# A ConvNeXt block whose convolution output is turned by VectorE out of PSUM, with the norm's mean and weights folded into the first matrix

## The chip, the cores and the metric

The kernel runs on one core of a Trainium2 chip. A core has five engines that run side by side, each through its own queue, in order: TensorE (PE, matrix products into PSUM, with a separate weight load, PEld), VectorE (DVE), ScalarE (ACT), GpSimd (POOL) and SyncE (SP, which here only issues DMAs). The metric is the device time of one launch in microseconds, the median of several runs. All data are 32-bit floats.

## The reference

The input is 32 images of 384 channels and 28 by 28 pixels. Cut to what matters:

```
y  = depthwise_conv_7x7(x, dw_w, padding 3) + dw_b        # each channel on its own
mu, var = mean and variance of y over the 384 channels, per pixel
y  = (y - mu) * rsqrt(var + 1e-6) * ln_g + ln_b
y  = gelu(y @ w1 + b1)                                    # 384 -> 1536
gx = sqrt(sum over pixels of y*y);  nx = gx / (mean over features of gx + 1e-6)
y  = grn_g * (y * nx) + grn_b + y
x1 = x + y @ w2 + b2                                      # 1536 -> 384
avg, mx, mn = mean, max, min of x1 over the pixels, per channel
out = sigmoid(small_gate(avg, mx, mn) + x1)
```

## The kernel before

**Convolution stage.** The 384 channels are walked in 48 steps (`s`) of 8 channels. An image is cut into 7 strips (`j`) of 4 rows, padded to 32 columns, so that a strip is 128 values; `turn_x` (L452) brings the strips onto the 128 partitions by 128x128 transposes on TensorE, and DVE or ACT copies them from PSUM into `xt`. For each channel `conv` (L580) multiplies all 7 x 32 = 224 strips by three blocks of a banded matrix `tmat` that holds the 49 weights (L599, L601, L603). The result of two channels lies in one PSUM bank, `pc` (4 banks rotate), with (row, column) of the strip on the partitions and (strip, image) along the free axis. One pair is read out by ACT (L615), the next by DVE (L607), each time adding the bias `dwb`, into `yc`, an SBUF tile of 16 channels (two buffers), which `store` (L623) writes to `yd` in DRAM every second step. SP issues, in order, the load of `tmat` three steps ahead (L406), the loads of x (L433), the stores of `yc` and the stores of `u` (L753).

In the same stage POOL forms two matrices in `form_w` (L518, lines L524 and L526): the two matrix products are carried out by schemes with fewer products, which multiply sums of weight blocks (`UPSTEPS`, `STEPS`) with sums of input blocks (`FORMS`, `SUMS`). `form_w` writes each sum of weight blocks into one of three `u` buffers and stores it to DRAM; u1 (from w1) is formed from step U1 = 4 on, u2 (from w2) from step U2 = 22 on. w1 and then w2 lie in the same tile, `ws`, into which `later` (L699, L700) loads them at steps 2 and 19.

**From conv to blocks.** The last two steps are done twice: first for images 0 to 15, then for images 16 to 31. Beside the second half, `first_image` (L653) normalises and transposes image 0.

**Per image.** `load_y` (L271) fetches one image, pixels of a strip on the partitions, strips and channels along the free axis. `block_stats`, `stats` and `std` (L289, L279, L294) take mean and variance on DVE; `norm` (L793) applies them on ACT, strip by strip; `turn` (L802) transposes each 128x128 piece on TensorE (L816, 7 strips x 3 blocks = 21); `evac` (L818) copies from PSUM on ACT, multiplies by `ln_g` and adds `ln_b`, into `room_acc`, channels on the partitions. `forms_up` (L320) makes the sums of input blocks on POOL. `up` (L836) multiplies by w1 in 15 steps for each of 4 groups (L858); ACT and DVE gather the products from PSUM (L865 to L875); ACT applies Gelu (L828), squares and sums (L834) and scales (L308 through `affine`). `down` (L962) multiplies by w2 in 38 steps of 6 products (L986), with the operands' sums on POOL (L947); DVE adds the products to the image's x (L1001, L1003) and takes max and min of each quarter of a channel (L1008). `gate_store` (L1021) ends an image.

**Order.** The main loop calls `up(b + 1)` and then `down(b)`. What runs beside them hangs on their steps by two tables: `within` (L1070) for `up`, `beside` (L1124) for `down`. A planner puts each engine's instructions in an order from its own time estimates; `keep_in_program_order` pins an instruction behind what was written before it on its engine, `issue_after` pins a load behind an earlier one. Each engine then works through its queue in that order.

## Time and profile before

| | |
|---|---|
| median of 3 runs | 3089.75 us (3089.39 to 3091.18) |
| profiled execution: its span, first to last instruction | 3087.8 us; the page gives no other time for this execution, so its own time stands here as its span, 1.95 us under the median |
| mean granted TensorE clock | 0.997 |
| convolution stage | to about 493 us |
| one image in the middle of the main loop | 80.33 us |
| DMA in the convolution stage (24 to 480 us) | 355 GB/s, share 0.94 |
| DMA in the main loop | 189 GB/s, share 0.59 |

The profile gives each engine's busy time, the groups of equal instructions with their mean duration, the waits (which instruction waited for which), and the chain that ended last: from the last instruction back, at each step, to what released it. Matrix products are pipelined: the durations of two in a row overlap, so the cost of one on the path is read from the distance of two starts. A 32-bit product is recorded as two instructions.

### The profile page before, as it was taken

To read this page: it belongs to the slowest core of one execution; us is meant where nothing else is said; L and a number is where in the kernel's file an instruction comes from. 1 tells how busy PE (TensorE), PEld (TensorE's weight loads), DVE (VectorE), ACT (ScalarE), POOL (GpSimd) and SP (SyncE) were. 2 spreads that over 40 slices of the span, in tenths; PEclk is the share of its full clock that TensorE was granted. 3 is DMA by queue.
4 is the path that set the end of the run, shared out by engine and by line. 5 is a ranking of instruction groups with operands and counts; after the bars stand their busy time and mean duration, and the time that the engine had idled before them with its cause. 6 is when DMAs were issued, how large, how long until landed. Compare 5 with 4: busy or idle time off the path is not lost.

```text
span 3087.8 us, 45729 instructions
## 1 busy us (share of the span) xinstructions
PE 3055.8 (99%) x15011; PEld 2484.8 (80%) x15011; DVE 1992.4 (65%) x5382; ACT 1982.9 (64%) x3147; POOL 2265.9 (73%) x1767
## 2 busy tenths in 40 slices
PE   8999999999999999999999999999999999999998
PEld 8999997777777777777777777777777777777777
DVE  3444446666667777776666676666666666666766
ACT  3333335757777777777777777777777777777761
POOL 1233442798888888888888888888888888888897
PEclk9999999999999999999999999999999999999999
DMA  9999986455555555556565666655565555555546
GB/s 370 368 373 349 356 325 230 137 157 190 189 191 189 191 191 191 190 189 198 190 197 190 197 191 196 194 186 182 188 195 180 184 185 189 190 189 191 187 153 201
DMA packets 316132, 658.31 MB, mean 213 GB/s; under 512 B 127583, under 2 KB 142202, under 8 KB 306938
## 3 DMA queue, kind: packets, MB, share of 16 engines
q1 hardware_dynamic: 302916, 616.59, 60.7%
q10 hardware_dynamic: 12982, 38.80, 3.2%
q8 instruction: 122, 2.00, 0.3%
q14 instruction: 112, 0.92, 0.1%
HBM read 560.78 MB, written 94.53 MB: 212 GB/s over the span
## 4 chain that ended last, share of the span: by engine, by line
PE 94%; POOL 3%; DVE 1%; ACT 1%; DMA 1%; issue 0%; ACTq 0%; SPq 0%; POOLq 0%; DVEq 0%
PE ph_A L858 13%; PE ph_C L858 13%; PE ph_B L858 13%; PE pz_A L986 8%; PE pz_C L986 8%; PE pz_D L986 7%; PE pz_F L986 7%; PE pc L599 5%; PE pc L603 4%; PE pc L601 4%; PE py L816 2%; PE pt L460 2%; PE pz_H L986 2%; PE pz_I L986 2%; PE pz_E L986 2%; POOL d_room L947 1%
## 5 line engine op out<-in xcount | busy, mean ns | idle before, releaser
L947 POOL TENSOR_TENSOR d_room<-y 128x588 f32<-128x588 f32 x253 | 363.5, 1443 | 335.3 <-PE pz_B L986 187.6
L308 ACT ACTIVATE y<-y,fv,gsc 128x784 f32<-128x784 f32 x372 | 359.0, 1030 | 380.1 <-DVE gsc L894 380.1
L828 ACT ACTIVATE y<-y,fv 128x784 f32<-128x784 f32 x384 | 350.2, 945 | 186.4 <-DVE y L873 164.4
L858 PE MATMUL ph_A<-room,ws 128*128 128x392 f32 x1240 | 461.2, 494 | 0.8 <-ACT te L865 0.4
L858 PE MATMUL ph_C<-room,ws 128*128 128x392 f32 x1240 | 462.0, 495 | 0.0
L858 PE MATMUL ph_B<-room,ws 128*128 128x392 f32 x1240 | 458.8, 492 | 1.3 <-DVE yc L607 1.3
L947 POOL TENSOR_TENSOR d_room<-d_room,y 128x588 f32<-128x588 f32 x308 | 441.2, 1437 | 16.7
L858 PEld LDWEIGHTS ph_C<-room,ws 128*128 128x128 f32 x1240 | 232.9, 190 | 179.8 <-DVE y L871 20.6
L858 PEld LDWEIGHTS ph_A<-room,ws 128*128 128x128 f32 x1240 | 233.0, 190 | 178.8 <-ACT te L865 13.2
L858 PEld LDWEIGHTS ph_B<-room,ws 128*128 128x128 f32 x1240 | 234.6, 190 | 164.8 <-issue 1.5
L947 POOL TENSOR_TENSOR d_room<-y,d_room 128x588 f32<-128x588 f32 x214 | 307.6, 1437 | 44.9 <-PE pz_A L986 18.0
L834 ACT ACTIVATE junk<-y 128x784 f32<-128x784 f32 x384 | 329.0, 857 | 7.9
L343 POOL TENSOR_TENSOR room<-room 128x392 f32<-128x392 f32 x300 | 300.8, 1020 | 11.8
L947 POOL TENSOR_TENSOR y<-y 128x588 f32<-128x588 f32 x180 | 258.6, 1437 | 7.1
L867 DVE TENSOR_TENSOR y<-y,ph_C 128x392 f32<-128x392 f32 x384 | 214.4, 559 | 27.3
L1008 DVE TENSOR_REDUCE stq<-x 128x1 f32<-128x196 f32 x768 | 228.2, 349 | 5.5
L869 DVE TENSOR_TENSOR y<-y,ph_B 128x392 f32<-128x392 f32 x256 | 137.5, 557 | 143.5 <-ACT y L828 119.4
L615 ACT ACTIVATE yc<-pc,dwb 128x224 f32<-128x224 f32 (+1 forms) x200 | 103.5, 619 | 192.4 <-PE pc L603 183.9
L599 PE MATMUL pc<-xt,tmat 128*128 128x224 f32 (+1 forms) x800 | 213.6, 349 | 5.1 <-ACT xt L471 3.6
L986 PE MATMUL pz_A<-d_room,u 128*128 128x196 f32 x1050 | 203.5, 330 | 0.0
L524 POOL TENSOR_SCALAR u<-ws 128x384 f32<-128x384 f32 (+1 forms) x53 | 66.6, 1261 | 186.0 <-DMA u2d<-u 133.3
L469 DVE COPY xt<-pt 128x512 f32<-128x512 f32 (+1 forms) x184 | 112.0, 618 | 134.5 <-PE pt L460 134.4
(241 smaller groups left out, 6650.6 us busy)
## 6 DMA issues: line engine op xcount, KB each, us to landing
u<-u2d SPq DMA_DIRECT2D x487, 384.0 KB, 3.4
ws<-u1d SPq DMA_DIRECT2D x384, 320.0 KB, 3.0
tmat<-fs SPq DMA_DIRECT2D x47, 1420.0 KB, 11.6
ws<-u2d SPq DMA_DIRECT2D x121, 384.0 KB, 3.4
yd<-yc SPq DMA_DIRECT2D x22, 1792.0 KB, 6.7
yi<-yd SPq DMA_DIRECT2D x31, 1232.0 KB, 8.0
x<-in_x SPq DMA_DIRECT2D x32, 1176.0 KB, 5.6
out<-x ACTq DMA_DIRECT2D x31, 1176.0 KB, 7.1
```

The costliest lines, as they stand in the source:

```text
L308: eng.activation(out, in_, AF.Identity, bias=add, scale=mul)
L343: tc.keep_in_program_order(eng.tensor_tensor(d, o[in0], o[in1], op))
L599: keep(nc.tensor.matmul(po, t[:, c, P : 2 * P], xc, start=True, stop=False))
L601: nc.tensor.matmul(lo, t[:, c, 2 * P : T0 + MW], after, start=False, stop=False)
L828: nc.scalar.activation(y, y, AF.Gelu, bias=b1_t[:, f : f + 1], scale=1.0)
L834: nc.scalar.activation(junk, ys[b][:, f, :], AF.Square, accum_out=ssqs[b][:, f : f + 1])
L858: nc.tensor.matmul(banks[t, bk][:, :NH], wts[t][:, i % UG, :], o[opnd], start=(first == 1), stop=True, skip_group_check=True,)
L867: nc.vector.tensor_tensor(d, d, p, ALU.add)
L869: nc.vector.tensor_tensor(d, d, p, ALU.subtract)
L947: nc.gpsimd.tensor_tensor(d[0], o[a][0], o[c][0], ALU.add if sign == "+" else ALU.subtract)
L986: nc.tensor.matmul(pz[:, :NQ4], wt[:, i % UD, t, :], o[opnd][0][:, t, :], start=(first and t == 0), stop=(t == KD - 1), skip_group_check=True,
L1008: nc.vector.tensor_reduce(stq[:, v, m, h : h + 1], xh, AX.X, op2)
```

## The change

The convolution result stays unbiased in PSUM, and DVE turns it there in blocks of 32x32 (`nc.vector.transpose`): a block (32 columns of a row x 32 images) becomes (32 images x 32 columns), so `yt` holds (row in the strip, image) on the partitions and (channel, strip, column) along the free axis. `yt` has 8 channels and one more plane, the running sum over channels, which DVE's `sums_y` writes once a step; `yt` has two buffers and is stored every step. ACT squares `yt` with the bias added; POOL adds four squared channels at a time to `ssum`. At the end of the stage `finish` makes the reciprocal standard deviation of every pixel from the two sums, once for each half of the images, and stores it in `rsd`. `load_y` then fetches an image with the channels already on the partitions (three DMAs), and one row of reciprocal deviations spread over all partitions (a fourth, `rb`). `normed` adds the bias and multiplies by `rb` on DVE, three instructions an image, in place of the statistics, `norm`, `turn` and `evac`. The mean is not subtracted: `center_w` multiplies w1 by `ln_g` and takes its column means away, which removes the mean from the product, and adds `ln_b @ w1` to `b1`. It runs at the ends of steps 4 and 5; w1 is loaded at step 3 instead of 2, `fv` and `cv` (bias and norm vectors) at steps 1 and 2 instead of 4 and 5, w2 at 21 instead of 19; U1 and U2 move from 4 and 22 to 6 and 24. `form_w` starts with an addition where it can. Pixels of an image are now ordered by row in the strip, so `down` reads x with a stride of 112; max and min are taken once per channel (the last image excepted). The new pool `rbp` has one buffer.

```diff
+    yd = dram.tile([P, C, YR], F32, name="yd")
+    rsd = [dram.tile([P, YR], F32, name=f"rsd_{i}") for i in range(2)]
...
         with tc.issue_after(last_u2[-1]) if last_u2 else ExitStack():
-            nc.sync.dma_start(yk[:, : NY - NLAST], yd[:, :, b, :])
-        nc.sync.dma_start(yk[:, NY - NLAST :], yl[:, :, b, :])
...
+            for cb in range(CB):
+                load_y_part(b, yi, cb, 0, P)
+        base = rsd[0 if b < B0 else 1]
...
+                offset=base.offset + b * YR,
+                ap=[[0, P], [B * YR, NQD], [1, YR]],
...
+    def load_y_part(b, yi, cb, p0, p1):
+        nc.sync.dma_start(
+            yi[p0:p1, cb],
+            yd.rearrange("(q b) c n -> b c q n", b=B)[b, cb * P + p0 : cb * P + p1],
+        )
...
+    def normed(b, cbs=range(CB)):
...
+        for cb in cbs:
+            nc.vector.scalar_tensor_tensor(
+                accs[b][:, cb].rearrange("p (r w) -> p r w", w=HW), rows(yis[b][:, cb]),
+                dwb_t[:, cb : cb + 1], rows(rbs[b]), ALU.add, ALU.mult,
+            )
...
-        U1, U2 = 4, 22
+        U1, U2 = 6, 24
...
+            todo = sorted(terms(text), key=lambda x: -x[0])
+            blks = [(sg, wv[:, :, int(k), m, :]) for sg, m, k in todo]
+            if len(blks) > 1 and blks[0][0] > 0:
+                (_, a), (sg, c) = blks[:2]
+                nc.gpsimd.tensor_tensor(t, a, c, ALU.add if sg > 0 else ALU.subtract)
+                del blks[:2]
+            else:
+                nc.gpsimd.tensor_scalar(t, blks[0][1], float(blks[0][0]), None, ALU.mult)
+                del blks[:1]
+            for sg, blk in blks:
+                nc.gpsimd.tensor_tensor(t, t, blk, ALU.add if sg > 0 else ALU.subtract)
             stores.append((dst, t))
...
+        def center_w(part):
...
+                        nc.tensor.matmul(
+                            pb[:, f : f + 1], w1r[:, cb, f * P : (f + 1) * P],
+                            lnb_t[:, cb : cb + 1], start=(cb == 0), stop=(cb == CB - 1),
+                        )
+                nc.vector.tensor_tensor(b1f, pb[:, :FB], b1_t, ALU.add)
+                for cb in range(CB):
+                    nc.vector.tensor_scalar(
+                        w1r[:, cb], w1r[:, cb], lng_t[:, cb : cb + 1], None, ALU.mult
+                    )
+                return
+            f0 = (part - 1) * 4 * P
+            pm = psx.tile([P, 4, P], F32, tag="pt", name=f"pm_{part}")
+            pm = pm.rearrange("p a b -> p (a b)")
+            for cb in range(CB):
+                nc.tensor.matmul(
+                    pm, less, w1r[:, cb, f0 : f0 + 4 * P], start=(cb == 0), stop=(cb == CB - 1)
+                )
+            for cb in range(CB):
+                w = w1r[:, cb, f0 : f0 + 4 * P]
+                nc.vector.tensor_tensor(w, w, pm, ALU.add)
...
-            cy = cc % YC
-            if c2 % 2:
-                nc.vector.tensor_tensor(
-                    yc[:, b0:b1, :, cy : cy + 2].rearrange("p b j c -> p c j b"),
-                    pc[:, :, : NJ * nb].rearrange("p c (j b) -> p c j b", j=NJ),
-                    dwb[:, cc : cc + 2].unsqueeze(2).unsqueeze(3).to_broadcast([P, 2, NJ, nb]),
...
+            cy = 2 * c2
+            nc.vector.transpose(yt[:, cy : cy + 2, :], pc[:, :, :N])
...
+            for ci in range(2):
+                nc.scalar.activation(
+                    sq[:, cy % SQ + ci, :], yt[:, cy + ci, :], AF.Square,
+                    bias=dwb[:, cc + ci : cc + ci + 1], scale=1.0,
...
-            else:
-                for ci in range(2):
-                    nc.scalar.activation(
-                        yc[:, b0:b1, :, cy + ci].rearrange("p b j -> p j b"),
-                        pc[:, ci, : NJ * nb].rearrange("p (j b) -> p j b", j=NJ),
...
+            if cy % SQ == SQ - 2:
...
+                    nc.gpsimd.tensor_tensor(ssum, ssum, sq, ALU.add)
...
+            nc.vector.tensor_reduce(
+                dst, yt[:, n0:n1, :].rearrange("p c n -> p n c"), AX.X, ALU.add
...
+        def finish(yt, part, s2, half):
...
+            sums_y(s1, yt, TC - SQ, TC + 1)
+            nc.vector.tensor_reduce(s2r, s2.rearrange("p c n -> p n c"), AX.X, ALU.add)
+            nc.vector.scalar_tensor_tensor(mu, s1, dws, part, ALU.add, ALU.add)
+            nc.vector.scalar_tensor_tensor(s1, mu, 1.0 / C**2, mu, ALU.mult, ALU.mult)
+            nc.vector.scalar_tensor_tensor(va, s2r, 1.0 / C, s1, ALU.mult, ALU.subtract)
+            nc.vector.tensor_scalar(va, va, 0.0, EPS, ALU.max, ALU.add)
+            nc.scalar.activation(s2r, va, AF.Sqrt)
+            rs = s1
+            nc.vector.reciprocal(rs, s2r)
+            nc.scalar.dma_start(rsd[half], rs)
+            return rs
...
+                for q in range(NQD):
+                    nc.tensor.matmul(
+                        pr[q // 2][:, q % 2], ident[:, q * B : q * B + 1].to_broadcast([P, P]),
+                        rs, start=True, stop=True,
                     )
...
+                        nc.vector.scalar_tensor_tensor(
...
+                            rows(yis[0][:, cb, 2 * i : 2 * i + 2]),
+                            dwb_t[:, cb : cb + 1], rows(pr[i]), ALU.add, ALU.mult,
...
+                forms_up(0, nc.vector)
...
+                        nc.vector.memset(
+                            pcs[i][:, ci, :N].rearrange("p (j b) -> p j b", b=B)[:, :, B0:], 0.0
+                        )
...
+                                (nc.sync, nc.scalar)[q % 2].dma_start(
+                                    yd[
+                                        q * B + b0 : q * B + b1,
+                                        (NK - 2 + i) * TC : (NK - 1 + i) * TC, :,
+                                    ],
+                                    y2[i][q * B + b0 : q * B + b1, :TC, :],
+                                )
...
+                                sums_y(y2[1][:, TC, :], y2[0], 0, TC + 1)
...
+                            sums_y(part, y2[1], 0, TC - SQ)
...
+                first_image(2 * PAIRS, firsts["y"])
+                if B0 < B:
+                    finish(y2[1], part, ssum, 1)
...
+                nc.sync.dma_start(yd[:, s * TC : (s + 1) * TC, :], yt[:, :TC, :])
+                yn = new_yt(f"yt_{s + 1}")
+                sums_y(yn[:, TC, :], yt, 0, TC + 1)
...
+                nc.vector.tensor_reduce(dws, dwb, AX.X, ALU.add)
+            if U1 - 2 <= s < U1:
+                for part in ((0, 1), (2, 3))[s - U1 + 2]:
+                    center_w(part)
...
-                xh = xt[:, m, h * NQ4 : (h + 1) * NQ4]
+                xh = xt[:, m, :].rearrange("p (j q w) -> p q j w", q=NQD, w=HW)[:, NQD - 1 - h]
...
-                for v, op2 in ((1, ALU.max), (2, ALU.min)):
-                    nc.vector.tensor_reduce(stq[:, v, m, h : h + 1], xh, AX.X, op2)
...
+                elif not any(left[m, x] for x in "abcd"):
+                    for v, op2 in ((1, ALU.max), (2, ALU.min)):
+                        nc.vector.tensor_reduce(
+                            st[:, v * CB + m : v * CB + m + 1], xt[:, m, :], AX.X, op2
+                        )
...
+                at((0, 18), normed, 1)
...
-            for j in range(NJ):
-                at((0, 20 + j), block_stats, b + 1, j)
-            at((0, 28), stats, b + 1)
-            at((0, 28), std, b + 1)
-        if 1 <= b and b + 1 < B:
-            for j in range(3):
-                at((2, 24 + 2 * j), norm, b + 1, j)
...
-            for i, jj in ((0, (0, 1)), (3, (2, 3)), (7, (4, 5)), (TURNED, (6,))):
-                for j in jj:
-                    at(i, turn, b + 2, j)
-                for j in {0: (3, 4), 3: (5, 6)}.get(i, ()):
-                    at(i, norm, b + 2, j)
-                if i in (3, TURNED):
-                    at(i, evac, b + 2, i // TURNED)
+            for cb in range(CB):
+                at(2 + 3 * cb, normed, b + 2, (cb,))
```

## The prediction

> **What bounds the kernel now.** I read the page's span and chain first, to see which engine ends last; then busy time by stretches, one in the convolution stage and one whole image of the main loop; then the groups and waits that the change touches.
>
> ```profile
> span 3087.8 us, 45729 instructions
> ...
> PE 94%; POOL 3%; DVE 1%; ACT 1%; DMA 1%; issue 0%; ACTq 0%; SPq 0%; POOLq 0%; DVEq 0%
> ```
>
> ```profile
> 24.00:480.00 456.00, 454.48 (x2905) 441.24 (x2904) 187.92 (x301) 165.13 (x277) 164.41 (x155) 1.00 0.94 355
> 1120.39:1200.72 80.33, 80.33 (x374) 63.08 (x374) 55.65 (x158) 57.30 (x92) 65.67 (x51) 1.00 0.59 189
> ```
>
> The columns are length, then PE, PEld, DVE, ACT, POOL busy, granted clock, DMA share, GB/s. TensorE is the path in both stages; the others have slack (POOL 14.7 us of an image, DVE 24.7). In the convolution stage DMA is nearly full too. Next, what one transpose and one narrow product cost on PE, read from start to start:
>
> ```profile
> 1160.07 1.16 PE L986 MATMUL pz_A<-d_room,u 128*128 128x196 f32 x6
> 1161.07 0.49 PE L816 MATMUL py<-ident,yn 128*128 128x128 f32 x3
> 1161.39 1.16 PE L986 MATMUL pz_C<-d_room,u 128*128 128x196 f32 x6
> ...
> 1173.34 0.28 PE L886 MATMUL pg<-gs,ones_f 128*128 128x1 f32 x2
> 1173.48 1.24 PE L986 MATMUL pz_H<-d_room,ws 128*128 128x196 f32 x6
> ```
>
> Three transposes take 0.32 us of the path, 0.107 each; a product one column wide takes 0.14. Last, the groups of the convolution stage, the shared work of DVE and POOL, and POOL's wait:
>
> ```profile
> L816 PE MATMUL py<-ident,yn 128*128 128x128 f32 x651 | 92.1, 273 | 0.2
> L607 DVE TENSOR_TENSOR yc<-pc,dwb 128x448 f32<-128x448 f32 x92 | 85.6, 932 | 143.4 <-PE pc L603 134.7 <-ACT yc L615 4.0 <-PE pt L460 1.9
> L469 DVE COPY xt<-pt 128x512 f32<-128x512 f32 x96 | 65.6, 683 | 89.3 <-PE pt L460 89.1
> L469 DVE COPY xt<-pt 128x384 f32<-128x384 f32 x88 | 48.2, 548 | 45.3 <-PE pt L460 45.3
> L947 POOL TENSOR_TENSOR y<-y 128x588 f32<-128x588 f32 x180 | 258.6, 1437 | 7.1
> L526 POOL TENSOR_TENSOR u<-u,ws 128x384 f32<-128x384 f32 x71 | 70.2, 1002 | 3.5
> ```
>
> ```profile
> POOL u L524 <- DMA u2d<-u: 133.3, 21, 33.2
> ```
>
> ```profile
> L301 DVE SCALAR_TENSOR_TENSOR nmr<-mv,rstd x32: 156/1174/1434, 484.0 to 2885.9; 128x7 f32<-128x7 f32 x32
> ```
>
> Transposes wait for nothing (idle 0.2 us). POOL spends 133 us waiting for a `u` buffer's store, which hurts nobody now. And a DVE instruction of 7 elements with two SBUF inputs takes 0.16 us when POOL is idle (484 us) but 1.17 in the median: it waits about 1.0 us for POOL.
>
> **Part by part.** *Main loop.* 651 transposes leave PE: 651 x 0.107 = -69.7 us, 2.25 an image, if PE stays the path. ACT loses 7 `norm` and 6 `evac`; DVE loses 7 block statistics (0.545), 7 aggregations, 18 of 24 reductions of 0.349, and gains 3 `normed` of 784 elements: 0.95 each by the 1.05 ns an element of the two COPY rows, plus 1.0 of waiting for POOL: 5.9 us. DVE ends some 6 us lighter. They stand behind steps 2, 5 and 8 of `down`, where DVE has about 16 additions of 0.355, 5.7 us in 11; 5.7 + 5.9 just fits, and a bank is reused 4 steps later, so PE waits 0 (bounds 0 and 1 us an image, 30 us). What is queued behind `normed` is DVE's reading of those banks, and PE behind it. [...] SP issues four loads for two at the start of `up`, 1 us more, beside a wait of 27 us for u1 buffers; bytes grow by 0.46 MB in 80 us at share 0.59. Strided x: 0, bounds -0.05 and +0.1 us an addition, hidden by DVE's slack.
>
> [...]
>
> *`center_w`, all on PE's path, since the convolution of the next step is pinned behind it.* Part 0: 36 products x 0.14 = 5.0. Part 1 must wait for DVE to scale w1: three TENSOR_SCALAR of 1536 at 1.07 ns an element (four of 384 took 1.65 us at 484 us) 4.9, the sum into b1f 0.2, and the last product of 512 columns, 0.86 (392 columns are 0.33 an instruction, two each): 6.0. Parts 2 and 3: 6 x 0.86 = 5.2. w1 is issued a step later and needed at the end of step 4; w2 landed 15.4 us after its issue (208.9 to 224.3), so w1, issued near 56, lands near 71.5 to 76 against a step end at 72.4: +1. Sum +17, bounds 11 and 25. `fv` and `cv` are small, earlier and precede it on SP.
>
> *Convolution steps, 9.76 us each on PE.* DVE: four block transposes of 448 elements from PSUM. None is in the trace; the COPY rows give 0.615, whose slope is 1.05 ns an element over a start of 0.14; the bounds are 0.47 (slope alone) and 1.08 (twice the slope). With two strips copied (2.46) and one `sums_y` of 2016 strided elements (2.25 by the same line; bounds 2.1 and 4.3, slope alone and twice the slope) DVE has 7.2 of 9.76. ACT: eight squares of about 0.34 (392 elements take 0.49) and two paddings of 0.86: 4.4. POOL: two additions of 896, 2.1 each (1.002 and 1.437 give 2.13 ns an element), and the forms: 96.7 us over 22 steps by the new order of terms, 4.4: 8.6 of 9.76. But a step's second form waits for a `u` store (three buffers, 1.73 forms a step; the store is issued behind the next step's `yd` store and takes a median 8.5 us), so POOL runs up to 9 us late. Behind that wait stand the square additions, behind them ACT (two `sq` buffers, 9.8 us of cover less the 2.4 of a pair), behind ACT the padding of x and PE's transposes, one half step ahead. I take +3; bounds 0 and 40. `yt` must be stored within a step: `yd` stores landed after 5.7 to 11.8 us, and four PSUM banks cover one step more: 0. Bytes are the same; the cover of everything here is PE's 9.76, and DMA share 0.94 leaves little.
>
> *From conv to blocks.* Now the second half starts near 480.7 and the first `up` product runs at 494.8, 14.1 later. After: DVE turns two pairs (to 3.2 us), then `finish`, held by POOL's late squares to 7, runs 8.9 less the first sum of 1.3 (sums 1.3 and 1.1, three two-input instructions at 1.4, 0.35, the root 0.5, a reciprocal of 224 at 5 ns from its 1- and 7-element rows 1.3): to 14.6; six more transposes, two sums, 7.1; six readings of 392 elements at 0.56, 3.4; one form, 0.5: 25.6. That is +11.5. Eight PSUM memsets and a sum ahead of the first half, +2; the second `finish` sits on DVE ahead of `up`'s additions and stops PE at its seventh step, +5. Sum +18.5, bounds 3 and 30.
>
> *First two images.* From 536 to 563 us the chain is ACT's; it loses six evacuations (3.5), three norms (1.8), a root and table load (1.6): -7, bounds -10 and 0.
>
> Sum: -69.7 + 17 + 3 + 18.5 - 7 = -38.2. Against the profiled span of 3087.8: 3049.6; the median of the runs stands 1.95 above it: 3051.6, say 3052.
>
> **Rivals.** *DVE becomes the bound of the convolution (slower).* At 1.08 per transpose and 4.3 per `sums_y` a step takes 4.3 + 2.46 + 4.3 = 11.1, 1.3 over PE, 46 times, +60: 3112. It decides from 0.8 us a step on. For it: neither operation is in the trace; against: the PSUM copies that are nearest run at half that price. *POOL holds the convolution.* One to two microseconds over 22 steps, 3072 to 3096; the mechanism is above, and the POOL waits speak for it; against, the cover of a step. *`normed` stops PE 1 us an image*: 3082. *The transposes were hidden anyway*: about 3119, only the additions remain; the idle time of 0.2 us and an image that is 80.33 of 80.33 PE speak against.
>
> **How the numbers follow.** About 0.2% (6 us) is what can be told from no change. Chances: my forecast 0.56 (faster); POOL 0.16 (0.07 faster, 0.04 same, 0.05 slower); DVE 0.15 (0.02, 0.01, 0.12); `normed` 0.10 (0.05, 0.02, 0.03); hidden 0.03 (slower). Faster 0.70, same 0.07, slower 0.23. The forecast's own range is 3030 to 3075, from its bounds taken together by about half; with DVE's rival 3028 to 3112.
>
> **What would show it.** Right: an image of 78.1 us, all PE; no L816; convolution steps of 9.76 but for 4 and 5; a gap of 5 to 6 us before part 1's products; the first `up` product some 25 us after the second half begins. Wrong: steps of 10.5 us or more with DVE or POOL busy above 95%; PE waiting for DVE's x additions in `down`; transposes of 1 us or more. What would upset it most is a block transpose slower than a copy.

## The result, and the profile after

After takes 3105.37 us (median of 4 runs, 3104.21 to 3106.15), before 3089.57 us (4 runs): ratio 1.005, 95% interval 1.0036 to 1.0064. The change made the kernel 16 us slower; the forecast was 3052 us, 38 us faster. The profiled execution of after has a span of 3103.9 us, 1.8 us under its own run time.

From the page of after, the span and the chain that ended last:

```profile
span 3103.9 us, 43870 instructions
...
PE 86%; DVE 6%; POOL 4%; DMA 2%; issue 1%; ACT 1%; SPq 0%; DVEq 0%; ACTq 0%; POOLq 0%
```

PE had 94% of the chain and has 86%; DVE went from 1% to 6%. By stretches (length, then PE, PEld, DVE, ACT, POOL busy, granted clock, DMA share, GB/s), the convolution stage and one image:

```profile
24.00:480.00 456.00, 438.28 (x2676) 416.53 (x2675) 342.39 (x393) 198.79 (x412) 276.38 (x188) 0.97 0.90 328
...
1128.00:1206.17 78.17, 77.99 (x354) 60.95 (x353) 52.16 (x125) 48.44 (x76) 66.22 (x51) 1.00 0.62 201
```

The image is 78.17 us and all PE, as forecast (78.1). The convolution stage is not: PE works 438 of 456 us at a mean clock of 0.97, where it worked 454 at 1.00. Cut into five stretches by events on PE, the two spans compare like this:

| stretch (us) | before | after | difference | forecast |
|---|---|---|---|---|
| start to the first product of step 6 | 81.7 | 114.0 | +32.3 | +17 |
| steps 6 to 45 | 389.0 | 404.4 | +15.4 | +3 |
| first half step to first `up` product | 24.1 | 43.7 | +19.6 | +13.5 |
| first `up` to first `down` product | 84.1 | 94.9 | +10.8 | +5 - 7 |
| from there to the end | 2508.9 | 2446.9 | -62.0 | -69.7 |
| sum | 3087.8 | 3103.9 | +16.1 | -38.2 |

The main loop gave 62 us; the first 657 us took 78, of which 31.5 were forecast.

**Where the first stretch went.** Granted clock of PE, microsecond by microsecond, around `center_w` (same columns; PE's busy time is the second number):

```profile
72.00:73.00 1.00, 0.30 (x3) 0.07 (x1) 1.00 (x3) 0.28 (x1) 0.00 (x0) 1.00 1.02 420
73.00:74.00 1.00, 0.00 (x0) 0.00 (x0) 1.00 (x3) 1.00 (x4) 0.00 (x0) 1.00 1.01 424
74.00:75.00 1.00, 0.00 (x0) 0.00 (x0) 1.00 (x3) 1.00 (x4) 0.54 (x1) 0.71 1.01 424
75.00:76.00 1.00, 0.00 (x0) 0.00 (x0) 0.26 (x1) 0.81 (x3) 1.00 (x1) 0.50 1.03 430
...
78.00:79.00 1.00, 0.88 (x5) 0.91 (x5) 0.00 (x0) 0.00 (x0) 0.69 (x1) 0.50 1.05 436
...
97.00:98.00 1.00, 1.00 (x2) 0.34 (x1) 1.00 (x1) 0.00 (x0) 0.00 (x0) 0.50 0.00 0
98.00:99.00 1.00, 1.00 (x4) 0.42 (x3) 1.00 (x1) 0.00 (x0) 0.00 (x0) 0.84 0.00 0
99.00:100.00 1.00, 1.00 (x8) 0.97 (x7) 1.00 (x3) 0.00 (x0) 0.00 (x0) 1.00 0.00 0
```

PE has nothing to do from 72.3 on, because w1 has not landed; at about 74.4 its clock is halved, and it stays halved until about 98.3, through all 36 narrow products and the first three wide ones:

```profile
78.12 15.49 PE L545 MATMUL pb<-cv,ws 128*128 128x1 f32 x72 [5.82 <-DMA ws<-in_w]
93.94 5.00 PE L559 MATMUL pm<-ws,less 128*128 128x512 f32 x6 [0.32 <-DVE ws L551]
```

Now the groups of after that the forecast had priced:

```profile
L545 PE MATMUL pb<-cv,ws 128*128 128x1 f32 x72 | 15.5, 352 | 5.8 <-DMA ws<-in_w 5.8
...
L669 DVE TENSOR_REDUCE yt<-yt 128x224 f32<-128x2016 f32 x46 | 170.2, 3701 | 4.4 <-DMA yd<-yt 3.7 <-ACT xpad L452 0.3
...
L646 DVE STREAM_TRANSPOSE yt<-pc 128x448 f32<-128x448 f32 x184 | 112.5, 632 | 42.3 <-PE pc L643 41.7
...
L308 DVE SCALAR_TENSOR_TENSOR room<-yi,cv,rb 128x784 f32<-128x784 f32 x90 | 111.9, 1244 | 0.0
```

The products take 15.5 us after a wait of 5.8; `sums_y` takes 3.70 us, not 2.25; the block transpose 0.632 (forecast 0.615); `normed` 1.24 (forecast 1.95 with the wait for POOL). POOL's longest waits answer the rival that it would hold the stage:

```profile
POOL ssum L663 <- ACT sq L651: 165.0, 49, 26.4
```

POOL waits for squares, and of the 133 us of waiting for a store of u2 0.2 are left. Last the timeline at the end of the stage (start, duration, engine, then in brackets the idle time ahead and its releaser):

```profile
554.60 3.35 PE L729 MATMUL pr<-xt,ident 128*128 128x224 f32 x8 [13.13 <-DVE xt L699]
562.11 2.95 PE L913 MATMUL ph_B<-room,ws 128*128 128x392 f32 x4 [4.15 <-DVE room L342]
...
577.91 2.98 PE L913 MATMUL ph_B<-room,ws 128*128 128x392 f32 x4 [8.52 <-ACT y L920]
...
577.36 0.89 ACT L920 ACTIVATE y<-ph_B 128x392 f32<-128x392 f32 x2 [8.10 <-DMA rsd<-xt]
```

PE stands 13.1 us for the first `finish` on DVE, 4.2 for the first forms, and 8.5 for ACT's first copies, which wait for the store of the second half's `rsd`.

### The profile page after: what moved, and what is told of

Its sections match the earlier page's. It is cut to its first block, busy times and chain, and to the rows that moved or that the text cites. A ratio compares the mean times of both kernels' runs of the same rounds, so it can differ in the third digit from the quotient of the medians.

```text
span 3103.9 us, 43870 instructions
## 1 busy us (share of the span) xinstructions
PE 3021.0 (97%) x14437; PEld 2441.4 (79%) x14437; DVE 2110.7 (68%) x4502; ACT 1772.9 (57%) x2886; POOL 2455.4 (79%) x1841
## 3 DMA queue, kind: packets, MB, share of 16 engines
q1 hardware_dynamic: 274340, 630.94, 61.8%
## 4 chain that ended last, share of the span: by engine, by line
PE 86%; DVE 6%; POOL 4%; DMA 2%; issue 1%; ACT 1%; SPq 0%; DVEq 0%; ACTq 0%; POOLq 0%
PE ph_C L913 13%; PE ph_A L913 12%; PE ph_B L913 11%; PE pz_A L1041 8%; PE pz_C L1041 8%; PE pz_F L1041 7%; PE pz_D L1041 7%; PE pc L639 4%; PE pc L641 3%; PE pc L643 3%; PE pz_H L1041 2%; PE pt L464 2%; PE pz_I L1041 2%; PE pz_E L1041 2%; POOL d_room L1002 2%; DVE room L308 2%
## 5 line engine op out<-in xcount | busy, mean ns | idle before, releaser
L883 ACT ACTIVATE y<-y,b1f 128x784 f32<-128x784 f32 x384 | 350.4, 945 | 206.7 <-DVE y L928 184.0
L663 POOL TENSOR_TENSOR ssum<-ssum,sq 128x896 f32<-128x896 f32 x95 | 198.8, 2093 | 167.5 <-ACT sq L651 165.0
L651 ACT ACTIVATE sq<-yt,dwb 128x224 f32<-128x224 f32 x376 | 152.7, 470 | 158.9 <-DVE yt L646 149.0
L639 PE MATMUL pc<-xt,tmat 128*128 128x224 f32 x736 | 202.9, 358 | 15.4 <-DVE yt L646 7.2
L1041 PEld LDWEIGHTS pz_A<-d_room,u 128*128 128x128 f32 x1050 | 178.8, 190 | 8.1 <-issue 0.6
L641 PE MATMUL pc<-xt,tmat 128*96 128x192 f32 x736 | 181.2, 328 | 0.0
```

What stands on the lines that cost most here:

```text
L639: keep(nc.tensor.matmul(po, t[:, c, P : 2 * P], xc, start=True, stop=False))
L641: nc.tensor.matmul(lo, t[:, c, 2 * P : T0 + MW], after, start=False, stop=False)
L651: nc.scalar.activation(sq[:, cy % SQ + ci, :], yt[:, cy + ci, :], AF.Square, bias=dwb[:, cc + ci : cc + ci + 1], scale=1.0,)
L663: nc.gpsimd.tensor_tensor(ssum, ssum, sq, ALU.add)
L883: nc.scalar.activation(y, y, AF.Gelu, bias=b1f[:, f : f + 1], scale=1.0)
L1041: nc.tensor.matmul(pz[:, :NQ4], wt[:, i % UD, t, :], o[opnd][0][:, t, :], start=(first and t == 0), stop=(t == KD - 1), skip_group_check=True,
```

## The experiments

Theory A: the main loop's gain is TensorE's 21 transposes an image; it is more than eaten by separate stalls ahead of it, which add up. Its rivals are named in each expectation. "Before" ran beside each kernel on the same chip (medians 3089.1 to 3090.1 us); differences to after are to 3105.4. This table cuts the profiled execution of each at the same events (us):

| kernel | median | to step 6 | steps 6 to 45 | half steps to `up` | `up` to `down` | rest |
|---|---|---|---|---|---|---|
| before | 3089.6 | 81.7 | 389.0 | 24.1 | 84.1 | 2508.9 |
| after | 3105.4 | 114.0 | 404.4 | 43.7 | 94.9 | 2446.9 |
| e1, w1 earlier | 3100.7 | 113.2 | 406.4 | 42.2 | 94.3 | 2448.5 |
| e11, vectors and w1 earlier | 3096.1 | 110.4 | 400.8 | 42.2 | 93.9 | 2445.6 |
| e2, no narrow products | 3092.2 | 99.2 | 404.2 | 45.6 | 95.3 | 2445.7 |
| e6, 12 narrow products | 3100.2 | 108.2 | 404.6 | 43.5 | 95.2 | 2446.2 |
| e3, no channel sums | 3083.9 | 113.9 | 388.9 | 39.0 | 93.9 | 2446.4 |
| e5, sums out of PSUM | 3087.5 | 115.6 | 389.2 | 41.9 | 92.7 | 2445.0 |
| e12, sum in four pieces | 3089.2 | 115.6 | 389.2 | 43.7 | 93.4 | 2445.0 |
| e13, sum behind two transposes | 3094.9 | 114.3 | 396.3 | 42.8 | 93.3 | 2445.8 |
| e4, a tile for the second `rs` | 3099.7 | 115.3 | 404.4 | 43.8 | 88.8 | 2445.6 |
| e7, transposes put back | 3183.6 | 113.7 | 406.3 | 42.2 | 94.3 | 2524.5 |
| e8, e4 + e5 + e6 | 3070.6 | 105.6 | 389.2 | 41.9 | 88.5 | 2446.5 |
| e9, e8 with `center_w` spread | 3065.1 | 99.2 | 389.2 | 42.0 | 88.5 | 2446.6 |
| e10, e9 with halves' sums out of PSUM | 3060.9 | 97.4 | 389.2 | 37.0 | 89.2 | 2446.4 |

### The main loop: transposes put back (e7)

```diff
+            for i, jj in ((0, (0, 1)), (3, (2, 3)), (7, (4, 5)), (TURNED, (6,))):
+                for j in jj:
+                    at(i, dummy, b + 2, j)
...
+        for cb in range(CB):
+            n = j % 4 * P
+            nc.tensor.transpose(dpts[b][cb][:, n : n + P], ones_f, ident)
```

> The computation is that of after, with 21 more transposes of 128x128 on TensorE an image, of a constant, into banks that nobody reads, at the four places where before had its own. Theory A (the image got shorter because TensorE has 21 transposes less): the image goes back from 78.2 to 80.2 to 80.6 us, in all 3164 to 3172 us. Theory B (it got shorter because ACT's and DVE's untwisting and statistics went, and TensorE had room for the transposes): the image stays under 79 us, in all under 3130 us.

Measured 3183.56 us, ratio to before 1.0303 (1.0288 to 1.0319). From the timeline of one image, and the whole image by stretches:

```profile
1403.43 0.49 PE L1090 MATMUL dm<-ident,ones_f 128*128 128x128 f32 x3
1403.76 1.16 PE L1041 MATMUL pz_C<-d_room,u 128*128 128x196 f32 x6
```

```profile
1400.00:1480.94 80.94, 80.28 (x375) 63.14 (x374) 53.19 (x124) 48.44 (x76) 66.18 (x51) 1.00 0.59 196
```

The image goes from 78.17 to 80.94 us, with DVE, ACT and POOL as light as in after. So TensorE's transposes are what an image is shorter by, not the relief of the others. Each takes 0.11 us from start to start, 2.3 of the 2.77 us. The other 0.5 is PE's waiting: 0.66 us of this image are idle and 0.18 of after's, both times ahead of one `ph_C` product that waits for DVE; over the main loop these waits come to 16.9 us against 2.6, about the 12 us by which the run lies above the band. Why DVE comes later there is not known.

### `center_w`: the wait for w1 (e1, e11)

e1 exchanges the places of the loads of w1 and of the small vectors `cv` in `later`; e11 loads `cv` in step 1, beside `fv`, and w1 in step 2.

```diff
-            3: (
+            2: (
                 ws.rearrange("p (cb f) -> p cb f", f=FF),
...
-            2: (cv, cvec.rearrange("v (cb p) -> p v cb", p=P)),
+            1.5: (cv, cvec.rearrange("v (cb p) -> p v cb", p=P)),
```

> Only the places of two loads are exchanged: the first matrix (w1) is loaded in conv step 2 and the small vectors in step 3; nothing is left out. Theory A (each loss found in the trace after stands alone and adds up: center_w 32 us, of it 5.8 us PE's wait for w1): w1 lands some 10 us earlier, before PE reaches the bias products at 72.3, so PE's wait of 5.8 us goes, and what hangs on it: 3097 to 3101 us against 3105.4. Theory B (the stalls of the first steps share one cover, the wall of the conversion tables' loads behind w1 on SP's queue, tmat landing at 92.87): nothing is won, 3104 to 3107 us.

> The kernel after with both small vectors loaded in step 1 and w1 in step 2, and nothing else; nothing is left out. Theory A (in e1 the small vectors, loaded behind w1, landed as late as w1 had, and held PE in its place): PE's wait of 5.8 us at the bias products goes, 3097 to 3101 us, and the 15.5 us of the products stay. Theory B (something else holds the products at 78 us): 3103 to 3106 us.

e1: 3100.74 us, ratio 1.0038 (1.0023 to 1.0053), runs from 3098.8 to 3106.3. The median lies in A's band, but A is not shown by it: the interval overlaps after's (1.0036 to 1.0064), and the profiled execution, the slowest of the four (3106.3 us), shows no gain. PE still waits 3.9 us there, and its products begin at 77.99 (after: 78.12). From the chain of e1:

```profile
63.31 14.54 DMA cv<-in_cvec
...
77.99 14.65 PE pb L545 x68
```

w1 was issued at 53.99 and landed at 69.0. The load of `cv`, a few bytes to each partition, landed 14.5 us after its issue, at 77.85, and the products need it. In after, issued ahead of w1, it took 9.5 us, so how much of the 14.5 is w1's doing is not shown. e11 takes that wait away too: 3096.1 us, 1.0018 (1.0008 to 1.0028), and PE comes straight from its transposes to the products. What the clock then does was expected by neither theory (stretches of e11):

```profile
74.00:75.00 1.00, 1.00 (x10) 0.98 (x9) 0.00 (x0) 0.00 (x0) 0.00 (x0) 1.00 0.81 294
...
76.00:77.00 1.00, 1.00 (x11) 1.00 (x11) 0.00 (x0) 0.00 (x0) 0.00 (x0) 1.00 1.02 430
77.00:78.00 1.00, 1.00 (x9) 1.00 (x8) 0.00 (x0) 0.00 (x0) 0.00 (x0) 0.73 1.03 433
78.00:79.00 1.00, 1.00 (x7) 1.00 (x6) 0.00 (x0) 0.00 (x0) 0.00 (x0) 0.50 1.08 460
```

They begin at 74.86 at full clock, without a gap, and at about 77.5 (the mean of 0.73 puts it at 77.46) the clock is halved although PE is never idle. They take 12.98 us instead of 15.49: at half clock a product costs 0.43 us (15.49 / 36), so the 10.4 us from 77.46 on hold 24 of them, and the first 12 took 2.6 us, 0.22 each. Only 3.6 us of e11's 9.3 lie in this stretch; 3.6 lie in steps 6 to 45, of them 2.6 in step 34, where after's PE waits 2.5 us (below) and e11's does not. That e11's earlier loads are the reason is not shown: step 34 takes 12.4 us in e1, e2 and e6 too.

### `center_w`: the narrow products (e2, e6)

e2 leaves out the share of `ln_b` in the first bias. e6 keeps the whole computation: DVE first adds the three blocks of w1, each weighted by its column of `ln_b`, and PE makes 12 products by a column of ones; the loads stand as in e11.

```diff
-                for f in range(FB):
-                    for cb in range(CB):
-                        nc.tensor.matmul(
-                            pb[:, f : f + 1], w1r[:, cb, f * P : (f + 1) * P],
-                            lnb_t[:, cb : cb + 1], start=(cb == 0), stop=(cb == CB - 1),
-                        )
-                nc.vector.tensor_tensor(b1f, pb[:, :FB], b1_t, ALU.add)
+                nc.vector.tensor_copy(b1f, b1_t)
```

```diff
+                for q in range(KT - 1):
+                    tq = ufp.tile([P, KT, P], F32, tag="uf", name=f"lb_{q}")
...
+                            nc.vector.scalar_tensor_tensor(tq, blk, c1, tq, ALU.mult, ALU.add)
...
+                            pb[:, f : f + 1], tq[:, i * P : (i + 1) * P], ones_f[:, :1],
+                            start=True, stop=True,
```

> Leaves out of the computation the share of norm's offset in the first bias: the 36 products of 128x128 by one column in center_w's part 0 (15.5 us of PE after); b1f is a copy of b1. Theory A (losses stand alone): PE's 15.5 us goes and the wait for w1 stays, so 3089 to 3092 us. Theory B (DVE's first scaling of w1 waits for tmat's landing at 92.87 as its row says, whatever PE does): the scaling, the part 1 products and the conv behind them begin where they did, under 3 us is won, 3102 to 3106 us.

> Nothing is left out: both small vectors are loaded in step 1 and w1 in step 2, and the 36 products of one column become 12, over the weighted sum of w1's three blocks that DVE forms first (three instructions of 512 a third of the row). Theory A (weights are what a product of one column pays for, 0.43 us each, and w1 came late): 12 products cost 5.2 us in place of 15.5 and the wait of 5.8 us is gone; DVE's nine pieces, some 4 to 5 us, lie in the wait for w1 in part: 3087 to 3095 us. Theory B (DVE's pieces, which the products now wait for, take the place of the products): 3098 to 3103 us.

e2: 3092.21 us, 1.0009 (0.9999 to 1.0019), at the upper end of A's band; the first stretch is 14.8 us shorter. DVE's scaling of w1, first in after and then in e2:

```profile
92.86 1.02 DVE L551 TENSOR_SCALAR ws<-ws,cv 128x1536 f32<-128x1536 f32 x1 [17.60 <-DMA tmat<-fs]
...
78.76 2.88 DVE L544 TENSOR_SCALAR ws<-ws,cv 128x1536 f32<-128x1536 f32 x3 [3.37 <-DMA ws<-in_w]
```

It starts at 78.76, when w1 has landed, and not at 92.86, so the landing of `tmat` that its row in after names was only the last event before it: it had waited for the products that read w1. A holds.

e6: 3100.2 us, 1.0034 (1.0021 to 1.0047): B, and the timeline of DVE shows how.

```profile
77.50 3.53 DVE L678 TENSOR_REDUCE yt<-yt 128x224 f32<-128x2016 f32 x1
80.94 2.23 DVE L655 STREAM_TRANSPOSE yt<-pc 128x448 f32<-128x448 f32 x4
83.10 0.71 DVE L551 SCALAR_TENSOR_TENSOR lb<-ws,cv,lb 128x512 f32<-128x512 f32 x1
```

The last of nine pieces stands behind a channel sum and four transposes, and PE waits 6.07 us for it; its clock is at 0.50 from 80 to 86 us, and step 6 begins 5.8 us earlier than in after. The products themselves were cheap (3.8 us); the place where DVE feeds them was not.

### Steps 6 to 45: the channel sum (e3, e5, e12, e13)

e3 leaves out the sum of the first 46 steps. e5 makes it out of PSUM, e12 cuts the reduce in four, each pinned behind a block transpose, e13 leaves it in one piece but pins it behind the second transpose of the next step.

```diff
-                sums_y(yn[:, TC, :], yt, 0, TC + 1)
+                nc.vector.tensor_copy(yn[:, TC, :], yt[:, TC, :])
```

```diff
             nc.vector.transpose(yt[:, cy : cy + 2, :], pc[:, :, :N])
+            if s < NK - 2:
+                if cc:
+                    nc.vector.tensor_tensor(acc, acc, pc[:, :, :N], ALU.add)
```

```diff
                     conv(s, c2, yt, xt, 0, B)
+                    if s:
+                        q = slice(c2 * YR // PAIRS, (c2 + 1) * YR // PAIRS)
+                        src = prev[:, :, q].rearrange("p c n -> p n c")
+                        keep(nc.vector.tensor_reduce(yt[:, TC, q], src, AX.X, ALU.add))
```

```diff
+                    if s and c2 == 1:
+                        src = prev.rearrange("p c n -> p n c")
+                        keep(nc.vector.tensor_reduce(yt[:, TC, :], src, AX.X, ALU.add))
```

> Leaves out of the computation the channel sums of conv steps 0 to 45 (46 reduces of 3.70 us each; a copy of 224 elements carries the sum row on), so the norm's mean is wrong; the last two steps keep theirs. Theory A (the reduce, 3.7 us where 2.25 was forecast, is what delays the block transposes and so PE in steps 6 to 45, 13.9 us longer than before): that stretch goes back to 388 to 391 us, in all 3088 to 3093 us. Theory B (the stretch is longer because the store of yt is late on SP's queue and holds the next buffer): most of it stays, 3099 to 3105 us.

> Nothing is left out: in conv steps 0 to 45 the channel sum is no longer a reduce over the transposed tile (3.70 us a step) but four adds a step of the bank that the transpose has just read to a running sum of 128x448, which is transposed once at the end. Theory A (the one block of 3.7 us on DVE holds back the transposes and so the four banks): four pieces of some 0.55 to 0.65 us, 2.2 to 2.6 us a step and each between two transposes, stop PE no more; steps 6 to 45 go back to 388 to 393 us and the whole to 3085 to 3092 us. Theory B (what counts is the DVE work of a step and that a bank is held longer): 2.4 us in place of 3.7 wins only a third of what leaving the sums out won, 3096 to 3101 us.

> Nothing is left out and DVE does the same work as in after: the reduce of a step is cut into four of 56 columns each, and one is pinned behind each of the next step's four block transposes. This tells the length of one piece from the work in sum, which e3 and e5 changed together. Theory A (one piece of 3.70 us between two steps holds back the four banks): four pieces of about 0.95 us hold nobody; steps 6 to 45 go back from 404 to 388 to 392 us and the whole to 3085 to 3093 us. Theory B (the sum of DVE's work with the two copies, 8.5 us of 9.76, is too much at any cut): steps 6 to 45 stay above 399 us, the whole 3100 to 3107 us.

> Nothing is left out and no work differs from after: the reduce of a step stays one piece of 3.70 us, but it is pinned behind the second block transpose of the next step instead of standing ahead of all four. Theory A (the place: ahead of the transposes it lets all four banks fill before the first is emptied): with two banks emptied first, PE does not wait, steps 6 to 45 take 388 to 393 us as with the reduce cut in four, the whole 3086 to 3093 us. Theory B (the length of the piece, wherever it stands, with the store of yt that it waits for): steps 6 to 45 stay above 399 us, the whole 3099 to 3106 us.

e3: 3083.94 us, 0.998 (0.9971 to 0.999). e5: 3087.52 us, 0.9994 (0.9985 to 1.0004). e12: 3089.18 us, 1.0 (0.9991 to 1.001). In all three the stretch is back at 389 us, before's length, so the stores of `yt`, the squares and POOL hold nothing there. The same stretch of before, after and e12 (same columns):

```profile
81.69:470.65 388.96, 387.44 (x2451) 375.85 (x2450) 160.04 (x247) 140.77 (x233) 152.35 (x142) 1.00 0.94 353
```

```profile
114.01:518.42 404.41, 392.68 (x2449) 377.72 (x2448) 319.45 (x365) 184.10 (x388) 284.87 (x196) 0.99 0.90 328
```

```profile
115.57:504.77 389.20, 387.80 (x2449) 375.54 (x2448) 332.58 (x483) 190.80 (x390) 284.15 (x196) 1.00 0.93 341
```

DVE works 333 us in e12's 389, more than the 319 in after's 404, and PE stands 1.4 us in place of 11.7. So it is not that DVE was full. Of after's 15.4 us, 10.2 are idle time and 5.2 are longer products (392.7 us against 387.4). Some 2.2 of these follow from 4.5 us of work at half clock after the longest wait (the mean is 0.67 from 450 to 455 us); the rest is not accounted for. The two longest waits:

```profile
403.52 0.65 PE L639 MATMUL pc<-xt,tmat 128*128 128x224 f32 x2 [2.49 <-DVE yt L646]
...
448.83 1.12 PE L639 MATMUL pc<-xt,tmat 128*128 128x224 f32 x2 [4.66 <-DVE yt L646]
```

The timeline of DVE ahead of the longer wait shows the order:

```profile
444.21 0.56 DVE L473 COPY xt<-pt 128x384 f32<-128x384 f32 x1 [1.70 <-PE pt L464]
444.69 3.54 DVE L669 TENSOR_REDUCE yt<-yt 128x224 f32<-128x2016 f32 x1
448.14 2.23 DVE L646 STREAM_TRANSPOSE yt<-pc 128x448 f32<-128x448 f32 x4
```

The reduce stood in DVE's queue behind copies that waited for PE and ahead of all four transposes; the four banks were full, and PE stood.

This did not happen in every step. By the starts of their first products, steps 6 to 21 take 156.7 us in after as in before, although each has the same reduce ahead of its transposes. The loss comes behind them, against before 2.7 us in step 34 and 8.0 in steps 38 and 39. What differs is DVE's order. In step 18, as in the others of these sixteen, copies lie between the transposes (in some the last two stand together):

```profile
232.23 3.71 DVE L669 TENSOR_REDUCE yt<-yt 128x224 f32<-128x2016 f32 x1
235.85 0.64 DVE L646 STREAM_TRANSPOSE yt<-pc 128x448 f32<-128x448 f32 x1
236.41 0.65 DVE L473 COPY xt<-pt 128x512 f32<-128x512 f32 x1
236.99 0.63 DVE L646 STREAM_TRANSPOSE yt<-pc 128x448 f32<-128x448 f32 x1
```

From step 23 on the planner has put two to four transposes in a row and up to six copies behind them, directly ahead of the reduce. Why its order changes there is not known, and no run keeps the early order to the end.

e12 changed the length of the piece and its place together, e13 the place alone: 3094.88 us, 1.0019 (1.0009 to 1.0028), 396.3 us for the stretch, 8 of the 15.4 us won. The sum hides two effects: steps 23 to 45 lie 2.6 us over e12's, where after's lay 15.6 over; but steps 6 to 21, where after had lost nothing, now take 161.5 us, 4.4 over e12's. Only the cut has neither loss. Neither theory of e13 holds by itself.

e3's median lies 4 us below A's band: 4.7 us are gained in the half steps, where DVE has a copy in place of the reduce of step 45. That this is the cause is argued, not shown.

### The transition: the second `rs` (e4)

```diff
+    rs_own = const.tile([P, YR], F32, name="rs_own")
...
-            rs = s1
+            rs = rs_own if half else s1
```

> The reciprocal of the second half goes into a tile of its own instead of a row of the room that the main loop's y and x tiles take over; nothing is left out. Theory A (ACT's first copy of up(0) and DVE's normed(1) wait 8.1 and 6.6 us for the store of that row to have read it, and PE waits 8.5 us for the copy): the wait goes, 3094 to 3098 us. Theory B (the other rows in that room, the half stores of y and finish's reads, end as late): under 3 us is won, 3102 to 3106 us.

3099.65 us, 1.0033 (1.0019 to 1.0046), 5.7 us off, a little short of A's 7 to 11. The same two rows in the timeline of e4:

```profile
573.61 2.47 PE L914 MATMUL ph_B<-room,ws 128*128 128x392 f32 x4 [2.83 <-ACT y L921]
...
573.06 0.89 ACT L921 ACTIVATE y<-ph_B 128x392 f32<-128x392 f32 x2 [2.41 <-DMA rb<-rsd]
```

PE's wait falls from 8.52 to 2.83 us, by just what the run gained. The store had not been slow work on anybody's path: its source lay in memory that the main loop's `y` takes over, so ACT could not write there until the store had read it. What stays is ACT's order: its first copies stand behind the square root of the second `finish` and the issue of its store, which waits for DVE's reciprocal (570.69 to 572.24). The load of `rb` that the row names landed only at 574.87, after the copy had begun; the chain of e4 runs from the reciprocal over that issue to the copy.

### All together, and two steps more (e8, e9, e10)

e8 is e4, e5 and e6 in one. e9 forms the weighted sums and scales w1 (now on ACT) at the end of step 3, makes the 12 products at the end of step 4 and the centring products at the end of step 5. e10 makes the sums of the half steps out of PSUM too.

```diff
-            if U1 - 2 <= s < U1:
-                for part in ((0, 1), (2, 3))[s - U1 + 2]:
+            if U1 - 3 <= s < U1:
+                for part in ((-1,), (0,), (1, 2, 3))[s - U1 + 3]:
                     center_w(part)
```

```diff
+                av, pv = (
+                    v.rearrange("p c (j b) -> p c j b", b=B)[:, :, :, b0:b1]
+                    for v in (acc, pc[:, :, :N])
+                )
+                nc.vector.tensor_tensor(av, av, pv, ALU.add)
...
-            sums_y(s1, yt, TC - SQ, TC + 1)
+            nc.vector.tensor_tensor(va, acc[:, 0], acc[:, 1], ALU.add)
+            nc.vector.transpose(s1, va)
```

> Nothing is left out: the running sum out of PSUM, the early loads with 12 products, and the reciprocal's own tile, all three together. Theory A (the losses lie one behind another and add up): their three gains together, some 13 to 18, 10 to 18 and 6 us off 3105, so 3064 to 3076 us, under before. Theory B (one cover under them, the transition or the loads on SP's queue, eats a part): 3080 to 3092 us.

> Nothing is left out. The three changes together as before (e8), and center_w spread over the ends of steps 3, 4 and 5: DVE's weighted sums and the scaling of w1 (now on ACT) at the end of step 3, the 12 products of one column at the end of step 4, the centring products at the end of step 5. Theory A (in e8 PE stood because its products were issued right behind the DVE work that feeds them): only PE's own time stays, some 3.8 us for the 12 products and 7.7 us for the centring, and center_w costs 12 to 15 us in place of e8's 23.5: 3058 to 3064 us. Theory B (DVE's 13 us of extra work in three steps is the limit wherever it is put): 3067 to 3072 us.

> Nothing is left out. The kernel e9, and in the two half steps too the channel sums are added up out of PSUM (half a bank each, some 0.35 us) in place of the reduces of 3.7, 3.5, 2.1, 2.1, 1.7 and 1.7 us. Theory A (the hole in PE between the half convolutions and up(0), 20.9 us in e8, is DVE's chain of reduces in two finishes): it shrinks by 6 to 12 us and the second finish ends earlier too, 6 to 14 us under e9. Theory B (POOL's sums of squares and the loads behind them end the hole): under 3 us from e9.

e8: 3070.64 us, 0.9939 (0.9925 to 0.9954): the three gains by themselves, 5.7, 17.9 and 5.2 us, sum to 28.8, and e8 lies 34.7 under after: no cover under them ate a part. Where the 5.9 us beyond the sum come from is not known. e9: 3065.08 us, 0.9916 (0.9898 to 0.9934), a microsecond over A's band: the first stretch is 17.5 us over before's, since the clock still goes to half for nearly 7 us (0.50 from 78 to 84), behind 8 of the 12 products and the waits of 1.0 us ahead of them and 1.5 us after them. e10: 3060.9 us, 0.9905 (0.9887 to 0.9922), the fastest, 29 us under before; only 4.2 under e9, less than A asked. The stretch from the half steps to `up` shrank from 42.0 to 37.0 us:

```profile
516.03 3.35 PE L755 MATMUL pr<-xt,ident 128*128 128x224 f32 x8 [8.47 <-DVE xt L725]
523.54 2.95 PE L930 MATMUL ph_B<-room,ws 128*128 128x392 f32 x4 [4.15 <-DVE room L343]
533.94 1.58 PE L930 MATMUL ph_B<-room,ws 128*128 128x392 f32 x4 [3.69 <-ACT y L937]
```

The wait for the first `finish` is 8.5 us instead of 13.0 in e9; the second is that of e4 and e9 (4.15), the third is 3.7 us where both had 2.8.

## Why the prediction was wrong

Forecast and result lie 54.3 us apart: 15.3 in `center_w`, 12.4 in the convolution steps, 6.1 up to the first `up` product, 12.8 from there to the first `down` product and 7.7 in the main loop. The gain was priced about right; the costs ahead of it were not.

- *Main loop, -69.7*: right in mechanism (e7), 62.0 in size. An image lost 2.16 us, not 2.25 (0.103 a transpose, not 0.107), and I counted 31 images, of which one lay ahead of this stretch; a few images near its ends took 78.7. `normed` cost 3.7 us an image on DVE, less than the 5.9 forecast: in the middle images two of the three took 1.03 us with POOL idle, and one about 1.65 behind an addition of POOL. PE waited about 0.2 us an image behind it. The planner put it at the end of `up`, not behind steps 2, 5 and 8.
- *`center_w`, +17*: measured +32.3, and this is the largest miss. Part 0 was priced at 36 x 0.14 us = 5.0 from a single narrow product (L886), whose weight load had begun under the product before it (PEld at 1173.17, the product at 1173.34). In the row of 36 PEld was busy throughout (1.00 at 76 us of e11), and a product took 0.22 us at full clock, 7.8 in all. The clock was at 0.50, and they took 15.5; even without the wait ahead of them they took 13.0 (e11), where the clock fell to 0.50 2.6 us after their start with PE never idle. The wait for w1, taken as 1 us, was 5.8: w1 landed 15.1 us after its issue (forecast 15.4), but was issued at 62.86 and not near 56. Part 1, under the same clock, took 5.0 us for three wide products instead of 2.6, but the gap of 5 to 6 us ahead of it, named as a sign of being right, was 0.32. Parts 2 and 3 took 5.15 (forecast 5.2).
- *Conv steps, +3*: measured +15.4. The transpose was right (0.632 for 0.615); `sums_y` was not, 3.70 for 2.25, inside its bounds of 2.1 and 4.3. Even so DVE's sum, 2.5 + 2.5 + 3.7 = 8.7 us, fits into 9.76, and e12 does the same work at no loss. The step that failed is the budget itself: I compared work with time, and asked of each piece neither how long it holds the queue nor what stands behind it. Where the planner kept copies between the transposes the budget was right (steps 6 to 21, no loss). The +3 was priced for POOL's lateness, which did not show.
- *Conv to blocks, +18.5*: measured +19.6 up to the first `up` product (forecast 13.5; from the start of the second half 32.0 us, forecast 25.6, before 14.1), and then PE's wait of 8.5 us at the fourth step of `up` (forecast 5 at the seventh). The second `finish` does stop `up`, through the memory of its result and through ACT's queue, not through DVE's additions. The chain of the first `finish` was too short: its reduces took 1.7 to 3.7 us, a sum of the second half (3.5) stood ahead of it, and its two-input instructions took 1.6 and 1.9 us beside POOL (forecast 1.4). With the sums out of PSUM (e10) 12.9 of the 19.6 us are left, for which I have no run.
- *First two images, -7*: not to be found. The stretch from the first `up` to the first `down` product, in before and in after:

```profile
494.79:578.91 84.12, 83.02 (x263) 47.55 (x264) 63.60 (x141) 64.42 (x116) 27.05 (x22) 1.00 0.47 153
...
562.11:657.05 94.94, 84.84 (x242) 47.65 (x243) 67.37 (x119) 59.24 (x106) 27.01 (x22) 0.93 0.47 152
```

The step that failed is the reading of the chain: that it runs over ACT from 536 to 563 us was taken as time that a lighter ACT would save, but PE stood only 1.1 of these 84.1 us, so there was no such time to win. In after ACT is 5 us lighter and PE stands 10.1 us, 8.5 of them in the wait of the point above; PE's work, 21 transposes fewer, is 1.8 us longer at a mean clock of 0.93. e4's cure wins 6.1 of the 10.8 us.

- *Rivals.* DVE as the bound of the convolution came nearest in its place, but its mechanism (1.08 us a transpose, a DVE fuller than PE) did not occur. POOL held nothing. `normed` stopped PE by a fifth of the microsecond priced. The transposes were not hidden (and their 3119 left out the 1.95 us between span and median; it should read 3121).

## What to carry to other kernels

A new instruction on an engine with slack is not free by its sum: ask how long one piece holds the in-order queue, and what stands behind it that empties the buffers of the bounding engine; and look at the order in every step, for the same piece of 3.70 us cost nothing in sixteen steps and 8 us in two. Ask who takes over the memory of a result that a transfer still reads: here PE stood 8.52 us behind it, and 2.83 with a tile of its own (e4). Look twice at narrow products on a path that TensorE bounds: in the row of 36 one took 0.22 us at full clock (e11) and 0.43 at 0.50 (after), where one alone had taken 0.14 (before), and in after the three wide products behind them took 5.0 us at a mean clock of 0.56, where six at full clock took 5.15.

## What the runs showed of the hardware

- In after TensorE's clock fell to 0.50 about 2.1 us after its last product (72.3 to 74.4) and came back about 4.4 us into wide products (93.9 to 98.3); in between it had run 15.5 us of products one column wide without a gap. In e2 it fell 3.2 us after the last product (72.7 to 75.9) and came back 2.8 us into wide ones (79.9 to 82.7). In e11 it fell from 1.00 to 0.50 2.6 us after the first product of one column, with PE never idle, and came back 5.3 us into wide ones (89.2 to 94.5). The lengths at half clock, read from the means of the windows, were 23.9 us in after (74.4 to 98.3), 17.1 in e11 (77.5 to 94.5), and 6.8 in e2 (75.9 to 82.7) and in e9 (77.4 to 84.2). What sets these times no run shows.
- A reduce that reads with a stride of 896 bytes took 3.70 us for 2016 elements and 1.02 for 504, some 1.8 to 2.0 ns an element; one that reads 784 in a row took 0.963, 1.2 ns. No run here changes the stride alone.
- Two-input DVE instructions of 224 elements took 0.34 to 0.39 us when POOL was idle and 1.6 to 1.9 beside its additions of 2.09 us; of 784 elements 1.03 when POOL was idle and 1.24 in the mean of the main loop. POOL was held too: the addition behind such an instruction took 2.04 us at 1128.6 us of after, and the same addition 1.44 at 1143.0 us of before.
- The load of `cv` (7.5 KB) took 14.5 us from issue to landing in e1, about as long as w1 (2304 KB, 15.0 us) that was issued 9.3 us ahead of it, and 9.5 us in after. In after the DMA share from 52.3 to 61.8 us, where its `cv` was under way, was 1.00; no run tells which of the loads beside it held the small one.
